# Weights of the single blocks of a mixture of experts: a second place for the first halves, and an earlier start

## The chip, the cores and the metric

One core of a Trainium2 chip runs the whole program. The metric is the time of one execution in device microseconds (us): the kernel before took 1871.33, the median of three runs (1870.01 to 1871.95). Everything is float32.

The names in the profile: PE is TensorE's matmuls and PEld its weight loads, DVE is VectorE, ACT ScalarE, POOL GpSimd, and SP SyncE, which does nothing here but issue transfers. An "SPq" line is an instruction in SP's queue. "L1367" is line 1367 of the kernel.

## The reference

There are 32 sequences of 112 tokens (3584 tokens in all) with 256 channels, and for each sequence 375 rows of context. The layer has two residual steps:

```python
x = x + tanh(g_xattn) * cross_attention(ctx, layernorm(x))   # 16 heads of 64
x = x + tanh(g_ffn) * moe(layernorm(x))

def moe(x):                                  # D = 256, F = 1024, E = 8 experts
    s = softmax(x @ gate_w)                  # (T, E)
    top2, idx = top_k(s, 2); top2 /= sum(top2)
    h = gelu(x @ w1[e] + b1[e])              # w1 (E, 256, 1024), exact gelu
    y = h @ w2[e] + b2[e]                    # w2 (E, 1024, 256)
    return sum over the two experts of top2 * y
```

The cross-attention takes its queries from the normed x, and keys and values from the normed context with the normed x behind it. Only the mixture of experts (`moe`) is touched by the change, and of it only the last part.

## The kernel before

**Order.** Nothing is scheduled by a planner around the change: each engine runs its instructions in the order in which the code writes them, and semaphores hold an instruction back until what it needs is done. A transfer is an instruction in the queue of the engine that issues it (SP, ACT or POOL), so it also stands in that engine's order; a transfer that must wait for its place in SBUF to come free holds up everything behind it in that queue.

**Stages.** The attention of the sequences comes first and takes most of the time. Each of the 3584 tokens then belongs to two experts, which makes 7168 rows; the rows are written to DRAM (`xg`) sorted by expert, padded so that the parts below line up. While the last sequences are still in attention, the kernel works out which expert each part of 256 or 128 rows belongs to (`locate_early`, `locate_late`), and the experts' rows are gone through in two kinds of units:

- 21 *pairs* (t = 0 to 20, `PAIRS = 21`): two 128-row blocks of one expert at a time, 256 rows. Both layers use a scheme with seven block products instead of eight, for which sums of the weights were written to DRAM before (`ws1`, `ws2`). One pair takes 12.94 us on PE when nothing is waited for.
- 18 *single blocks* (t = 21 to 38, `SURE = 18`) of 128 rows, called block 0 to block 17 here, in order of the experts; three more exist under a condition on a register (`tc.If(more)`).

For each unit a table in DRAM holds three numbers that are read into registers by `number(m, i, column, ...)`: the expert, the row in `xg`, and a flag that is 1 where the expert is another than that of the unit before (column 2). The flag becomes `cond` of the fetches of weights: where it is 0 the fetch is skipped, as the weights are in place.

**A single block.** `hidden(t)` (L1360 to L1376) is layer 1 in 8 features of 128, each with two matmuls (L1367) and one gelu on ACT (L1374) that adds the bias b1. `turn_rows(t + 1)` (L1158) transposes the next block's rows. `second(t - 1)` (L1382) is layer 2 of the block before: 8 matmuls of 256 columns into one bank. `combine(t - 1)` adds b2 (DVE, L1232), scales each row by its gate (DVE, L1234), and sends the rows by a scatter-add to the output in DRAM (POOL, L1207, called "the add" below). So PE's order is: hidden layer of block t, transposes for t + 1, second layer of t - 1, and so on.

**Weights of a single block.** The two layers of an expert are 1 MB each. They come in halves of 512 KB: the first half of a layer serves its features 0 to 3, the second half 4 to 7. Each half has one place in SBUF, which is taken over from the pairs' weights:

| half | place (tile) before | read by PE at |
|---|---|---|
| layer 1, first | `s23` | L1367, features 0 to 3 of `hidden` |
| layer 1, second | `12_22` | L1367, features 4 to 7 |
| layer 2, first | `t14`, under the name `b1x` | L1382, first 4 matmuls of `second` |
| layer 2, second | `b2x` | L1382, last 4 matmuls |

The profile leaves numbers out of names: `w_s` is `s23`, `w` is `12_22`, `w_t` is `t14`, `w_b2x` is `b2x`. All four are fetched on SP's queue, in `fetch_first` (layer 1, L1119) and `fetch_second` (layer 2, L1135). Such a fetch waits until PE has done with the block before in that place, and what stands behind it on SP waits too. The biases are fetched on ACT's queue (`fetch_biases`: b1 at L1074, b2 at L1077, broadcast to all 128 partitions), into two places each by turns, and so are the rows (`fetch_rows`, L1057), three units ahead (`AHEAD = 3`). The order in `run()` before, for each block t:

```python
hidden(t)
fetch_first(t + 1); turn_rows(t + 1)
second(t - 1); combine(t - 1)
fetch_second(t)
rows_ahead(t, end)
```

So layer 1 of a block is fetched when the hidden layer of the block before has let go of the places, and layer 2 of block t when the second layer of block t - 1 has. Block 0's weights come the same way: layer 1 behind the hidden layer of pair 20 (t = 20), layer 2 behind pair 20's second layer. The loop over the pairs (L1854 to L1877) has the same form, with `hidden_pair`, `second_pair` and more kinds of planes per unit.

**Two places that were free by then.** `found["w1"]` (8 KB per partition, 1 MB) holds layer 1 of pair 0, and `w2_first` (L1138, the same size, in the attention's tile `exs[2]`) layer 2 of pair 0. Both are read for the last time while pair 0 is worked on (L1185 and L1200), and are not used after that.

Of the kernel before, what the change touches and what calls it, by code (L numbers as in the profile page):

```python
# [13 lines left out]
ET = mybir.EngineType  # L14
# [9 lines left out]
def kernel(  # L24
# [20 lines left out]
    nc = tc.nc  # L45
# [155 lines left out]
    if True:  # L201
# [861 lines left out]
        def expert_of(t):  # L1063
            m, i = unit_of(t)
            e = number(m, i, 0, E - 1, (ET.SP, ET.Activation) if t > 1 else (ET.SP,))

            new = {} if t in (0, 1, EARLY, PAIRS) else {"cond": number(m, i, 2, 1)}
            return e, new
# [31 lines left out]
        def fetch_first(t):  # L1100
# [3 lines left out]
            if t < PAIRS:  # L1104
                s1_, s4_ = (
                    (n, ws1[bass.ds(e, 1), place].rearrange("o p f -> p (o f)"))
                    for n, place in (("s1", 3), ("s4", 2))
                )
                s23 = "s23", ws1[bass.ds(e, 1), 0:2].rearrange("o s p f -> p (o s) f")
                order_ = (  # L1110
                    ("11", half_of_w1(e, 0, 0)), s23, s1_, ("12_22", rows_of_w1(e, 1)), s4_
                )
            else:
                if t == PAIRS:
                    wt["11"], wt["12"] = (wt["s23"][:, n] for n in range(2))
                    wt["21"], wt["22"] = (wt["12_22"][:, n] for n in range(2))
                order_ = ("s23", columns_of_w1(e, 0)), ("12_22", columns_of_w1(e, 1))
# [3 lines left out]
        def fetch_second(t):  # L1121
# [3 lines left out]
            if t < PAIRS:  # L1125
                planes = ws2[bass.ds(e, 1)].rearrange("o (a b) p c d -> b p (o a) (c d)", b=2)
                order_ = ("b11", half_of_w2(e, 0, 0, P)), b2x, ("t14", planes[0]), ("t32", planes[1])
            else:
                if t == PAIRS:
                    wt["b1x"] = wt["t14"].rearrange("p a f -> p (a f)").rearrange(  # L1130
                        "p (c d) -> p c d", d=D
                    )
                order_ = ("b1x", half_of_w2(e, 0, 0, D)), b2x
# [6 lines left out]
        def second_ahead():  # L1140

            e, _ = expert_of(0)
            nc.sync.dma_start(w2_first, w2[bass.ds(e, 1)].rearrange("o (c p) d -> p (o c) d", p=P))

# [216 lines left out]
        def hidden(t):  # L1361
            hid[t] = found["tiles"].tile([P, NF, P], F32, tag="h", name=f"h_{t}")
            for f in range(NF):
                ps = psum(P)
                h, c = divmod(f, NF // 2)
                for k, w in enumerate((("11", "12"), ("21", "22"))[h]):
                    nc.tensor.matmul(  # L1367
                        ps,
                        lhsT=wt[w][:, c * P : (c + 1) * P],
# [8 lines left out]
        def second(t):  # L1378
            ps = psy[t, 0] = psum(D, hold=(t, 0))
            for f in range(NF):  # L1380
# [4 lines left out]
                    rhs=wt[("b1x", "b2x")[h]][:, c, :],  # L1385
# [558 lines left out]
```

## Time and profile before

| | us |
|---|---|
| median of three runs | 1871.33 |
| the profiled execution, its own time | 1865.82 |
| its span, first to last instruction | 1864.0 |
| PE busy in the span | 1843.0 |
| DVE busy | 1377.0 |
| ACT busy | 1131.8 |
| POOL busy | 969.0 |

The mean granted clock of TensorE is 0.999 of full speed, so no time goes to a throttled clock. By the page's table of DMA queues 462.51 MB go through the queues, and the core's 16 DMA engines move a mean of 248 GB/s. Block 0's hidden layer runs at 1711 us of the span, between the two layers of pair 20; pair 20's second layer ends at 1722, and the last matmul of block 17 at 1856.

How to read the lines that follow: in a *timeline* a line gives start and length in us, then the engine, the line of the kernel, the operation, output<-inputs, and how many instructions were put together (x16); in the bracket stands how long the engine had been idle before and what ended that. In a table of *stretches* a line gives the stretch, its length, then busy time and number of instructions of PE, PEld, DVE, ACT and POOL, then the granted clock, the busy share of the DMA engines and the GB/s that they moved.

### The profile page before, as it was taken

The numbers are of one execution on the slowest core, as the hardware profiler recorded it, in microseconds if no ns is written. First come the engines' busy times: TensorE is split into PE (matmuls) and PEld (weight loads), VectorE is DVE, ScalarE is ACT, GpSimd is POOL, SyncE is SP. The second block draws the span as 40 slices with busy tenths as digits, with TensorE's granted clock in tenths as the row PEclk, the third lists the DMA queues.
The fourth block names the chain that finished last, engine by engine and source line by source line (L and its number), as shares of the span: only waits on it lengthen the run. The fifth ranks groups of instructions, "written<-read, shape, count | busy, mean of one in ns | idle before, by whom it ended". The sixth has DMA issues, their size and how long they took to land. (4 is left out here: it accounts for less than half of the span.)

```text
span 1864.0 us, 37204 instructions
## 1 busy us (share of the span) xinstructions
PE 1843.0 (99%) x12336; PEld 1410.6 (76%) x12336; DVE 1377.0 (74%) x2898; ACT 1131.8 (61%) x2718; POOL 969.0 (52%) x1361
## 2 busy tenths in 40 slices
PE   8999999999999999999999999999999999999998
PEld 4667777676677677767677767777677999999887
DVE  6888887888887878788878787888776477754111
ACT  4776666666676767676767676766656344434333
POOL 6433342525354846484556655662334688877212
PEclk9999999999999999999999999999999999999999
DMA  6577767666878888989898988897548876997872
GB/s 207 203 248 250 246 215 235 222 225 205 257 272 252 305 271 275 284 283 306 275 282 276 283 289 285 261 311 241 211 171 295 269 218 179 283 347 213 247 187 42
DMA packets 389747, 462.51 MB, mean 248 GB/s; under 512 B 142984, under 2 KB 279472, under 8 KB 373168
## 3 DMA queue, kind: packets, MB, share of 16 engines
q1 hardware_dynamic: 359568, 432.19, 70.0%
q0 software_dynamic: 11328, 15.33, 4.2%
q10 hardware_dynamic: 18656, 12.58, 2.5%
q8 instruction: 99, 1.62, 0.4%
q14 instruction: 96, 0.79, 0.1%
HBM read 316.05 MB, written 186.96 MB: 270 GB/s over the span
## 5 line engine op out<-in xcount | busy, mean ns | idle before, releaser
L592 ACT ACTIVATE ex<-bank,nmx 128x512 f32<-128x512 f32 x512 | 344.0, 698 | 86.2 <-DVE nmx L583 86.2
L606 ACT ACTIVATE ex<-ex,rc 128x512 f32<-128x512 f32 x512 | 345.1, 730 | 59.4 <-DVE rc L603 58.8
L583 DVE TENSOR_REDUCE nmx<-bank 128x1 f32<-128x487 f32 x512 | 298.3, 655 | 69.8 <-PE bank L573 69.3
L611 DVE STREAM_TRANSPOSE ex<-ex 128x1024 f32<-128x1024 f32 x256 | 314.1, 1227 | 20.3 <-ACT ex L606 20.2
L524 POOL TENSOR_TENSOR vv<-tmpv,vv 128x512 f32<-128x512 f32 x64 | 82.0, 1281 | 403.9 <-ACT vv L512 393.1
L573 PE MATMUL bank<-kT,qTs 64*128 64x487 f32 x1024 | 234.2, 583 | 0.8 <-ACT outT L652 0.3
L635 PEld LDWEIGHTS bank<-exT,vv 128*64 128x64 f32 (+1 forms) x4096 | 197.5, 136 | 29.5 <-issue 24.8
L652 ACT COPY outT<-bank 128x256 f32<-128x256 f32 (+3 forms) x160 | 40.0, 314 | 289.1 <-PE bank L635 289.1
L635 PE MATMUL bank<-exT,vv 128*64 128x112 f32 (+1 forms) x4096 | 211.3, 260 | 0.0
L471 PE MATMUL bank<-tT,wkv_s 128*128 128x487 f32 x378 | 186.5, 576 | 0.5 <-ACT ex L592 0.5
L476 PE MATMUL bank<-wkv_s,tT 128*128 128x256 f32 x768 | 186.5, 379 | 0.0
L476 PEld LDWEIGHTS bank<-wkv_s,tT 128*128 128x128 f32 x768 | 145.8, 190 | 44.0 <-issue 22.5
L1452 POOL TENSOR_TENSOR piece<-piece 128x128 f32<-128x128 f32 x256 | 117.2, 458 | 109.6 <-DMA piece<-in_L_ffn_w_dram 98.3
L573 PEld LDWEIGHTS bank<-kT,qTs 64*128 64x128 f32 x1024 | 98.4, 186 | 95.8 <-issue 70.7
L1207 POOL DMA_INDIRECT out_dram<-y,xs x60 | 93.6, 1559 | 148.7 <-DVE y L1234 64.8
L476 PEld LDWEIGHTS bank<-wkv,kvT 128*128 128x128 f32 x512 | 95.8, 190 | 56.3 <-issue 33.4
L476 PE MATMUL bank<-wkv,kvT 128*128 128x256 f32 x512 | 131.7, 380 | 0.8 <-ACT ex L592 0.6
L471 PE MATMUL bank<-kvT,wkv 128*128 128x487 f32 x252 | 130.1, 598 | 0.0
L521 DVE TENSOR_TENSOR vv<-bank,vv 128x512 f32<-128x512 f32 x192 | 123.4, 668 | 6.9 <-POOL vv L524 6.9
L521 DVE TENSOR_TENSOR kT<-bank,kT 128x487 f32<-128x487 f32 x189 | 116.8, 640 | 15.5 <-PE bank L471 15.2
L1262 ACT ACTIVATE h<-h,b 128x256 f32<-128x256 f32 x160 | 66.1, 495 | 89.5 <-DVE h L1275 89.5
L410 PEld LDWEIGHTS bank<-kvT,wq_sb 128*128 128x128 f32 x512 | 96.8, 190 | 28.1 <-issue 17.0
(299 smaller groups left out, 3654.9 us busy)
## 6 DMA issues: line engine op xcount, KB each, us to landing
turned<-ex SPq DMA_DIRECT2D x128, 1024.0 KB
exT<-turned SPq DMA_DIRECT2D x128, 1024.0 KB
w_t<-ws SPq DMA_DIRECT2D x40, 512.0 KB
w<-in_L_ffn_w_dram SPq DMA_DIRECT2D x38, 512.0 KB
w_b2x<-in_L_ffn_w_dram SPq DMA_DIRECT2D x38, 512.0 KB
ws<-piece SPq DMA_DIRECT2D x64, 256.0 KB
turned_in<-inputs SPq DMA_DIRECT2D x28, 512.0 KB
kvT<-turned_in SPq DMA_DIRECT2D x224, 64.0 KB
```

Source lines behind the costliest of these rows:

```text
L410: nc.tensor.matmul(ps, lhsT=wq_sb[:, k, i * P : (i + 1) * P], rhs=kvT[g][:, k, :, :S], start=(k == 0), stop=(k == KD - 1),)
L471: nc.tensor.matmul(ps, lhsT=w[:, 0, i * P : (i + 1) * P], rhs=x[:, :NK], start=True, stop=True)
L476: nc.tensor.matmul(ps[:, c, :], lhsT=x[:, (2 * h + c) * P : (2 * h + c + 1) * P], rhs=w[:, 1, i * P : (i + 2) * P], start=True, stop=True,)
L521: nc.vector.tensor_tensor(v[o], ps, v[r], ALU.add)
L573: nc.tensor.matmul(ps[:, :NK], lhsT=qT[b // 2, i][r, b % 2].rearrange("p a i -> p (a i)"), rhs=kT[b, i][r, :], start=True, stop=True,)
L583: nc.vector.tensor_reduce(nmx[b, i][:, j : j + 1], pss[b, i][j][:, :NK], AX.X, ALU.max, negate=True)
L592: nc.scalar.activation(exs[n % EXB][:, :, p, :, j, :], ps[j].rearrange("p (c r k) -> p k c r", c=NCK, r=QW), AF.Exp, bias=nmx[b, i][:, j : ...
L606: nc.scalar.mul(t, t, rc[:, j : j + 1])
L611: nc.vector.transpose(t, t)
L635: nc.tensor.matmul(ps[y * DH : (y + 1) * DH, r, x * S : (x + 1) * S].rearrange("p (a i) -> p a i", a=QB), lhsT=vv[j // 2, c // 2][:m, c % ...
L1207: add = nc.gpsimd.indirect_dma_start(out=outf, out_offset=bass.IndirectOffsetOnAxis(ap=xs[t][:, b, D + 1 : D + 2].bitcast(I32), axis=0), i ...
L1452: nc.gpsimd.tensor_tensor(o, l, r, op) for o, l, r, op in ops
```

## The change

Single blocks no longer use `fetch_first` and `fetch_second`; these keep the pairs alone. In their place:

- `single(t)` reads the registers of block t and says where its weights lie. First halves of both layers have two places by turns: those of even blocks lie in `room[:, 0]` (in `found["w1"]`) and in the first half of `w2_first`, those of odd blocks in `s23` and `b1x` as before. Second halves keep one place each (`12_22`, `b2x`), but for block 0, whose second halves lie in the other halves of `room` and `w2_first`.
- `fetch_single(t, layer, h)` sends one half. A second half is skipped where the block's expert is that of the block before, as now; a first half, whose place last held the block before that, is skipped only where both flags, of block t and of block t - 1, are 0. Blocks 0 and 1 are always fetched.
- In the pair loop block 0's four halves go out at t = 18 (`PAIRS - 3`), behind the layer-2 planes of pair 18; block 1's layer-1 halves go out at t = 20, where block 0's layer 1 went out before.
- In `run()`, behind `hidden(t)`: the second half of layer 1 of block t + 1, then the first half of layer 1 of block t + 2. Behind `combine(t - 1)`: the second half of layer 2 of block t, then the first half of layer 2 of block t + 1. b1 of block t + 1 goes out where it did, b2 of block t + 1 where b2 of block t did, so one block earlier.

Matmuls, gelus, the work on DVE and the adds stay as they are. The instructions of the single blocks in SP's queue grow by the eight further fetches that the looser condition lets through and by the arithmetic that joins the two flags.

```diff
@@ -1064,7 +1064,7 @@
             m, i = unit_of(t)
             e = number(m, i, 0, E - 1, (ET.SP, ET.Activation) if t > 1 else (ET.SP,))
 
-            new = {} if t in (0, 1, EARLY, PAIRS) else {"cond": number(m, i, 2, 1)}
+            new = {} if t in (0, 1, EARLY) else {"cond": number(m, i, 2, 1)}
             return e, new
 
         def fetch_biases(t, e, pool, n, layers=(0, 1)):
@@ fetch_first @@
...
-            else:
-                if t == PAIRS:
-                    wt["11"], wt["12"] = (wt["s23"][:, n] for n in range(2))
-                    wt["21"], wt["22"] = (wt["12_22"][:, n] for n in range(2))
-                order_ = ("s23", columns_of_w1(e, 0)), ("12_22", columns_of_w1(e, 1))
...
@@ fetch_second @@
...
-            else:
-                if t == PAIRS:
...
-                order_ = ("b1x", half_of_w2(e, 0, 0, D)), b2x
...
@@ -1141,6 +1128,30 @@
 
             e, _ = expert_of(0)
             nc.sync.dma_start(w2_first, w2[bass.ds(e, 1)].rearrange("o (c p) d -> p (o c) d", p=P))
+
+        def single(t, cond=True):
+
+            i = t - PAIRS
+            e = number("c", i, 0, E - 1, (ET.SP, ET.Activation))
+            one = two = {}
+            if cond and i > 1:
+                one = number("c", i, 2, 1)
+                one, two = {"cond": one}, {"cond": one | number("c", i - 1, 2, 1)}
+            H = NF // 2
+            room = found["w1"].rearrange("p k (h f) -> p h k f", h=2)
+            b1x = wt["t14"].rearrange("p a f -> p (a f)").rearrange("p (c d) -> p c d", d=D)
+            wt["w1", t] = [(room[:, 0], wt["s23"])[i % 2], wt["12_22"] if i else room[:, 1]]
+            wt["w2", t] = [(w2_first[:, :H], b1x)[i % 2], wt["b2x"] if i else w2_first[:, H:]]
+            found["one", t] = e, two, one
+
+        def fetch_single(t, layer, h):
+            e, *new = found["one", t]
+            dst = wt[("w1", "w2")[layer], t][h]
+            src = columns_of_w1(e, h) if layer == 0 else half_of_w2(e, h, 0, D)
+            nc.sync.dma_start(dst, src, **new[h])
+
+        def biases_of_single(t, layer):
+            fetch_biases(t, found["one", t][0], found["weights"], 2, (layer,))
 
         def weights_ahead():
 
@@ -1363,10 +1374,10 @@
             for f in range(NF):
                 ps = psum(P)
                 h, c = divmod(f, NF // 2)
-                for k, w in enumerate((("11", "12"), ("21", "22"))[h]):
+                for k in range(KD):
                     nc.tensor.matmul(
                         ps,
-                        lhsT=wt[w][:, c * P : (c + 1) * P],
+                        lhsT=wt["w1", t][h][:, k, c * P : (c + 1) * P],
                         rhs=xsT[t][:, k, 0, :],
                         start=(k == 0),
                         stop=(k == KD - 1),
@@ -1382,7 +1393,7 @@
                 nc.tensor.matmul(
                     ps,
                     lhsT=hid[t][:, f, :],
-                    rhs=wt[("b1x", "b2x")[h]][:, c, :],
+                    rhs=wt["w2", t][h][:, c, :],
                     start=(f == 0),
                     stop=(f == NF - 1),
                 )
@@ -1854,9 +1865,15 @@
         for t in range(1, PAIRS):
             if t > 1:
                 hidden_pair(t)
-                fetch_first(t + 1)
                 if t + 1 < PAIRS:
-                    found["next", t + 2] = expert_of(t + 2)
+                    fetch_first(t + 1)
+                    if t + 2 < PAIRS:
+                        found["next", t + 2] = expert_of(t + 2)
+                else:
+                    biases_of_single(PAIRS, 0)
+                    single(PAIRS + 1)
+                    fetch_single(PAIRS + 1, 0, 0)
+                    fetch_single(PAIRS + 1, 0, 1)
                 turn_rows(t + 1, nc.scalar.copy)
                 if t + 1 < PAIRS:
                     rows_sums(t + 1)
@@ -1871,6 +1888,11 @@
             if t + AHEAD == EARLY:
                 do(outgoing)
                 del outgoing[:]
+            if t == PAIRS - 3:
+                single(PAIRS)
+                for layer in range(2):
+                    for h in range(2):
+                        fetch_single(PAIRS, layer, h)
             rows_ahead(t)
             for _ in range(2 if t == 2 or t + AHEAD > EARLY - 3 else int(t > 1)):
                 do(outgoing[:1])
@@ -1881,17 +1903,28 @@
             for t in range(begin, end):
                 hidden(t)
                 if t + 1 < end:
-                    fetch_first(t + 1)
+                    if t > PAIRS:
+                        fetch_single(t + 1, 0, 1)
+                    biases_of_single(t + 1, 0)
+                if t + 2 < end:
+                    single(t + 2)
+                    fetch_single(t + 2, 0, 0)
+                if t + 1 < end:
                     turn_rows(t + 1)
-                    if t + 2 < end:
-                        found["next", t + 2] = expert_of(t + 2)
                 if t == PAIRS:
                     second_pair(t - 1)
                     out_pair(t - 1)
+                    biases_of_single(t, 1)
                 else:
                     second(t - 1)
                     combine(t - 1)
-                fetch_second(t)
+                if t > PAIRS + 1:
+                    fetch_single(t, 1, 1)
+                if t + 1 < end:
+                    fetch_single(t + 1, 1, 0)
+                    biases_of_single(t + 1, 1)
+                if t == PAIRS:
+                    fetch_single(t + 1, 1, 1)
                 rows_ahead(t, end)
             second(end - 1)
             combine(end - 1)
@@ -1902,8 +1935,11 @@
         with tc.If(more):
             for t in range(PAIRS + SURE, PAIRS + NS):
                 fetch_rows(t)
-                fetch_first(t)
-                fetch_second(t)
+                single(t, False)
+                for layer in range(2):
+                    biases_of_single(t, layer)
+                    for h in range(2):
+                        fetch_single(t, layer, h)
                 turn_rows(t)
                 hidden(t)
                 second(t)
```

More of the change, by code (lines that the diff above doesn't have):

```diff
@@ L1103, in fetch_first @@
             fetch_biases(t, e, found["weights"], 2, (0,))
[L1104 to L1112, printed above, removed]
-            else:
-                if t == PAIRS:
-                    wt["11"], wt["12"] = (wt["s23"][:, n] for n in range(2))
-                    wt["21"], wt["22"] = (wt["12_22"][:, n] for n in range(2))
-                order_ = ("s23", columns_of_w1(e, 0)), ("12_22", columns_of_w1(e, 1))
+            s1_, s4_ = (
+                (n, ws1[bass.ds(e, 1), place].rearrange("o p f -> p (o f)"))
+                for n, place in (("s1", 3), ("s4", 2))
+            )
+            s23 = "s23", ws1[bass.ds(e, 1), 0:2].rearrange("o s p f -> p (o s) f")
+            order_ = (
+                ("11", half_of_w1(e, 0, 0)), s23, s1_, ("12_22", rows_of_w1(e, 1)), s4_
+            )
             for n, src in order_:
@@ L1124, in fetch_second @@
             b2x = "b2x", half_of_w2(e, 1, 0, D)
-            if t < PAIRS:
-                planes = ws2[bass.ds(e, 1)].rearrange("o (a b) p c d -> b p (o a) (c d)", b=2)
-                order_ = ("b11", half_of_w2(e, 0, 0, P)), b2x, ("t14", planes[0]), ("t32", planes[1])
-            else:
-                if t == PAIRS:
-                    wt["b1x"] = wt["t14"].rearrange("p a f -> p (a f)").rearrange(
-                        "p (c d) -> p c d", d=D
-                    )
-                order_ = ("b1x", half_of_w2(e, 0, 0, D)), b2x
+            planes = ws2[bass.ds(e, 1)].rearrange("o (a b) p c d -> b p (o a) (c d)", b=2)
+            order_ = ("b11", half_of_w2(e, 0, 0, P)), b2x, ("t14", planes[0]), ("t32", planes[1])
             for n, src in order_:
```

## The prediction

> **What bounds the kernel now.** I read the page's busy table first, then the stretches with their DMA share, then PE's timeline over the single blocks, then SP's, ACT's and POOL's timelines beside it. "Block n" is single block n (0 to 17), "pair n" a pair of blocks; 19 and 20 are the last pairs.
>
> The busy table: PE works in all but 21 us, and a gain can come from there alone.
> ```profile
> PE 1843.0 (99%) x12336; PEld 1410.6 (76%) x12336; DVE 1377.0 (74%) x2898; ACT 1131.8 (61%) x2718; POOL 969.0 (52%) x1361
> ```
> The stretches (length, busy time of PE, PEld, DVE, ACT, POOL, then clock, DMA share, GB/s): late pairs, the blocks up to 11, the blocks that fetch no weights, two dense pitches, pairs 18 and 19. The late pairs run the DMA engines full (1.03) and PE loses nothing; in the single blocks they are at 0.79 and PE loses 5 us.
> ```profile
> 1644.00:1696.00 52.00, 52.00 (x468) 52.00 (x468) 28.16 (x60) 22.53 (x56) 40.19 (x41) 1.00 1.03 328
> ...
> 1726.00:1816.00 90.00, 84.58 (x566) 77.42 (x565) 13.65 (x34) 30.90 (x89) 18.90 (x13) 1.00 0.79 217
> ...
> 1816.60:1845.60 29.00, 29.00 (x202) 27.34 (x201) 4.81 (x12) 11.77 (x32) 6.18 (x4) 1.00 0.29 51
> ...
> 1757.59:1766.29 8.70, 7.41 (x53) 6.79 (x51) 1.63 (x4) 3.30 (x9) 2.77 (x2) 1.00 0.96 275
> 1766.29:1773.61 7.32, 7.32 (x51) 6.91 (x52) 0.78 (x2) 2.59 (x8) 1.43 (x1) 1.00 1.06 347
> ...
> 1686.00:1701.00 15.00, 15.00 (x137) 15.00 (x136) 8.96 (x22) 5.91 (x14) 9.98 (x10) 1.00 0.70 197
> ```
> PE's timeline: where it waits, it is at the first matmul of a half of weights (in the bracket: idle time and what ended it; the 1785.90 wait names DVE, but that matmul needs nothing of that instruction, and the DMA landed then). The last two lines give the pitch of a block that waits for nothing: 7.24.
> ```profile
> 1732.14 2.02 PE L1367 MATMUL bank<-xsT,w 128*128 128x128 f32 x16 [0.73 <-DMA w<-in_L_ffn_w_dram]
> ...
> 1742.42 1.97 PE L1382 MATMUL bank<-w_t,h 128*128 128x256 f32 x8 [0.79 <-DMA w_t<-in_L_ffn_w_dram]
> ...
> 1753.73 2.02 PE L1367 MATMUL bank<-xsT,w_s 128*128 128x128 f32 x16 [0.27 <-DMA w_s<-in_L_ffn_w_dram]
> ...
> 1766.29 1.97 PE L1382 MATMUL bank<-w_t,h 128*128 128x256 f32 x8 [1.29 <-DMA w_t<-in_L_ffn_w_dram]
> ...
> 1785.90 2.02 PE L1367 MATMUL bank<-xsT,w_s 128*128 128x128 f32 x16 [1.00 <-DVE y L1234]
> ...
> 1801.79 2.02 PE L1367 MATMUL bank<-xsT,w_s 128*128 128x128 f32 x16 [1.16 <-DMA w_s<-in_L_ffn_w_dram]
> ...
> 1820.40 1.89 PE L1382 MATMUL bank<-w_t,h 128*128 128x256 f32 x8
> ...
> 1827.64 1.89 PE L1382 MATMUL bank<-w_t,h 128*128 128x256 f32 x8
> ```
> SP's timeline: 0.37 or 0.38 is a fetch that is issued, 0.07 or 0.08 one that is skipped since the expert is the block's before. So blocks 2, 3, 5, 6, 7, 9 and 11 have a new expert, the others from 1 on not. The second line is skipped at the moment its place is free; PE uses that place at 1823.86, 5.27 later: that is the time a fetch has.
> ```profile
> 1795.20 0.37 SPq L1119 DMA_DIRECT2D w_s<-in_L_ffn_w_dram  x1
> ...
> 1818.59 0.08 SPq L1119 DMA_DIRECT2D w_s<-in_L_ffn_w_dram  x1
> ```
> POOL's: the scatter-adds of the results. Each starts 0.74 after the one before has landed, 6.69 apart here ((1772.18 - 1732.04)/6), close to the pitch.
> ```profile
> 1732.04 1.55 POOL L1207 DMA_INDIRECT out_dram<-y,xs  x1 [5.67 <-DMA b<-in_L_ffn_b_dram]
> ...
> 1737.42 1.54 POOL L1207 DMA_INDIRECT out_dram<-y,xs  x1 [3.83 <-issue]
> ...
> 1772.18 1.54 POOL L1207 DMA_INDIRECT out_dram<-y,xs  x1 [6.02 <-DMA w_s<-in_L_ffn_w_dram]
> ```
>
> **What can be won.** From block 0's second layer (1726.01) to block 12's (1820.40) are 94.39 us, 12 pitches of 7.24 are 86.88: 7.51 lost. By pitch: first halves 0.96 (block 2), 0.51 and 1.46 (block 5), 1.24 (block 9), 1.40 and 0.19 (block 11), together 5.76; second halves 0.97 (block 2) and 0.43 (block 6); 0.35 in small change. Each counts a slow first matmul after the gap. Nothing else in the diff touches a wait of PE, so 7.5 us (0.4%) is the ceiling.
>
> **Part 1, two places for first halves.** SP issues them behind the second half of the block before, some 2 us after that block's hidden layer, 3.7 us of hidden and second layer short of a full pitch more than now: about 9 us ahead of use against 5.27. No first half in the trace took over 6.8 from issue to use, so the 5.76 go. But two places mean that a first half is skipped only where both of the last two experts are its own: blocks 4, 8, 10 and 12 now fetch first halves in both layers, 8 fetches of 512 KB more. In the ten pitches of blocks 1 to 10 SP issues 33 fetches instead of 26.
>
> What that asks of the DMA engines: a block without weights keeps them busy 0.29 x 7.24 = 2.1 us. The stretch 1726 to 1816 has 0.79 x 90 = 71.1, less 12.43 blocks x 2.1 = 26.1, leaves 45.0 for 28 fetches: 1.61 each. The late pairs give a lower price: 53.6 us, less 4 pairs x 4.2, over 24.5 fetches' worth of bytes: 1.50. Ten pitches then need 33 x 1.50 + 21 = 70.5 to 33 x 1.61 + 21 = 74.1 us, and at 7.24 they last 72.4: 97 to 102%, where it was 80%. The wait of the second halves is what is late next. They still have one place each, are issued when it is free, and have 5.26 (1820.38 to 1825.64). The layer-1 ones of blocks 5, 7, 9 and 11 come third behind both layer-2 fetches of the block before, all within 3.6 us. Now, the third of such a train (first halves of 9 and 11) and the one of block 5 in the dense pitch took 6.43, 6.59 and 6.78 from issue to use: mean 6.60, 1.34 too late. Four times: **5.4**. Bounds: 1.8 in all, if they land like today's second halves of these blocks (5.31, 5.55, 5.92, 6.03 by the landing records, 0.05 to 0.8 late); 11.8, if one more fetch (1.61) stands before each. I take the middle row because the count in a train stays three. The ten other second halves keep what two of them lose now: **1.4** (0 to 3).
>
> [...]
>
> **Part 2, b2 a block earlier.** ACT's fetch of b2 now goes to the slot that the combine of the block before last reads. ACT waits for DVE's L1232 (0.25 after the second layer's end, 0.42 long); behind it stand the issue of b2 and of the rows (0.35 each, with their register loads 1.3) and the eight gelus. They start about 2.1 after the hidden layer does, against 0.65 (1746.70, hidden layer at 1746.05). PE asks for the first gelu at 3.57, when the transpose takes its bank: hidden, with 1.1 left. That cover goes if the combine is late, and it waits for the add of two blocks before to have landed (its y slot; 1736.67 by the landing records against 1737.93, 1.26 to spare). Cost **0.7**, between 0 and some 12 (second rival).
>
> **Part 3, block 0's weights.** Four fetches (6.0 to 6.4 us) go out behind pair 18's, at about 1688. SP pays 4 x 0.7 and three register loads of 0.3; behind them stand the rows of block 0 (due at 1704.87, landed 1693.8 now), pair 20's first layer (skipped) and pair 19's. Between 1686 and 1701 the engines are idle 0.30 x 15 = 4.5 us; so 1.5 to 1.9 us spill over onto pair 19's last planes, which landed at 1706.78 and are due at 1708.66, 1.88 to spare: **0.3** (0 to 1.5). Block 1's weights take over the places and the time of block 0's, and have 10 us more: nothing, covered by pair 20. SP's added register arithmetic (some 0.4 per first half) lies in front of fetches with 9 us of time: nothing.
>
> **Sum.** -7.51 + 5.4 + 1.4 + 0.7 + 0.3 = +0.3 us. The profiled execution took 1865.82 (span 1864.0), 5.5 below the median of the three runs, 1871.33; the difference is put on the median: 1871.6. A measurement can tell 0.2%, 3.7 us, from no change.
>
> **Rivals.**
> Faster: the second halves land as today's (1.8, 0.5 for the others, nothing else): -5.2, 1866.1. For it: only two of today's 14 make PE wait, and the trains that delay them lose a member. Against: the engines go from 80% to full. Chance 0.25.
>
> Slower, by the adds: they are bound by their own landing. At share 1.03 one took 7.45 (started at 1701.21), a loop of 8.2. Beyond 7.24 the excess comes back each block, through y, DVE and ACT's new wait, to PE: at a loop of 8.6, 10 x 1.36 - 1.3 = 12.3 stand in place of the weights' waits: +5.1, 1876.4. It decides from about 8.4; below, slower pitches give the weights the time that they lack. For it: 6.69 leaves 8%. Against: 1688.28 landed after 6.13 in the full late pairs. Chance 0.20.
>
> Slower, by the queue: one more fetch ahead of each train: 11.8 + 1.4 + 1.0 - 7.5 = +6.7, 1878.0. For it: 102%. Against: PE's waits drain the queue. Chance 0.13.
>
> The change not doing what it says: a first half could still wait for PE. The order of SP's instructions shows them without a wait on PE past the second half ahead of them, so I leave it at nothing.
>
> **How the numbers follow.** My case, within 0.2% of before: 0.42, 1871.6, by itself 1868 to 1875. Faster 0.25, slower 0.33. Range 1865.8 to 1877.5: it holds my case, the faster rival and the first slower one, and cuts the second's outer half.
>
> **What would show it.** Right: no PE wait on the two alternating places; waits at second halves of layer 1 in blocks 5, 7, 9, 11; DMA share near 0.9 from 1726 on; 0.37 issues for first halves of blocks 4, 8, 10 and 12. Wrong: block pitches of 7.24 throughout (then the engines had room), or gelus that PE waits for (then the adds bind).

## The result, and the profile after

The changed kernel is slower: 1880.91 us median against 1871.26, ratio 1.0061 with a 95% interval of 1.0050 to 1.0072 (the two medians alone are 9.65 us, 0.52%, apart). That is above the range that was given (1865.8 to 1877.5), and on the other side of the likeliest case.

The profiled execution took 1883.44 us, its span 1881.7. Against the span before (1864.0) it is split at three places that every profile of these kernels shows: the start of pair 19's group of 24 matmuls in layer 1, the start of block 0's hidden layer, and the starts of the second layers of blocks 0 and 12.

| stretch | before | after | difference |
|---|---|---|---|
| start of the span to pair 19's x24 group | 1686.57 | 1690.36 | +3.79 |
| from there to block 0's hidden layer ("pair stretch") | 24.78 | 30.12 | +5.34 |
| block 0's hidden layer to its second layer | 14.66 | 14.67 | +0.01 |
| block 0's second layer to block 12's ("block stretch") | 94.39 | 103.27 | +8.88 |
| from there to the last group of matmuls | 33.94 | 33.94 | 0.00 |

The first row lies in the attention and the earlier pairs, which the change does not touch; other profiles (below) have anything from 1687.79 to 1694.73 there, a second one of the kernel before 1690.46. So in this profile the change costs 5.3 us at the pairs' end and 8.9 in the blocks; the forecast had 0.3 and 0. Together that is more than the times show: 9.65 us by the medians, 11.4 by the ratio, 9.2 by the ratio of e11 below. The pair stretch comes again almost to the tenth (30.04 in a second profile), so by the times the blocks' part is some 4 to 6 us. The runs e1 and e4 below leave the blocks as the change has them, and lost 3.75 and 4.69 there.

The busy table after, and the stretches that were read before (the columns are the same):

```profile
PE 1850.6 (98%) x12336; PEld 1414.8 (75%) x12336; DVE 1377.4 (73%) x2898; ACT 1123.0 (60%) x2718; POOL 969.5 (52%) x1361
```
```profile
1644.00:1696.00 52.00, 52.00 (x467) 51.94 (x466) 29.81 (x64) 21.68 (x53) 39.96 (x41) 1.00 1.05 339
1686.00:1701.00 15.00, 15.00 (x137) 15.00 (x136) 7.33 (x16) 6.71 (x17) 11.80 (x15) 1.00 0.99 303
1700.00:1726.00 26.00, 23.05 (x188) 22.46 (x187) 10.13 (x24) 9.25 (x25) 13.62 (x12) 0.93 0.72 212
1726.00:1816.00 90.00, 79.44 (x534) 72.66 (x533) 14.19 (x36) 22.96 (x82) 19.63 (x13) 0.98 0.85 233
```

PE has as many matmuls as before and is busy 7.6 us longer: some of them are slower, and the granted clock is 0.93 and 0.98 in two stretches that had 1.00. The idle share of the DMA engines between 1686 and 1701 is used up (0.99, it was 0.70), as forecast. In the blocks the share is 0.85, where the forecast had "near 0.9", and yet PE loses 10.6 us of 90.

PE's timeline after, the waits at the pairs' end and in the blocks:

```profile
1710.16 1.13 PE L1328 MATMUL bank<-w_b,h 128*128 128x128 f32 x8 [1.12 <-DMA w_b<-in_L_ffn_w_dram]
1712.53 1.16 PE L1328 MATMUL bank<-w_b2x,h 128*128 128x128 f32 x8 [1.23 <-DMA w_b2x<-in_L_ffn_w_dram]
1714.29 1.97 PE L1328 MATMUL bank<-w_t,h 128*128 128x128 f32 x8 [0.60 <-DMA w_t<-ws]
1716.05 1.91 PE L1328 MATMUL bank<-w_t,hs 128*128 128x128 f32 x8
...
1749.33 2.02 PE L1378 MATMUL bank<-xsT,w 128*128 128x128 f32 x16 [1.53 <-DMA w<-in_L_ffn_w_dram]
...
1762.74 1.99 PE L1393 MATMUL bank<-w_b2x,h 128*128 128x256 f32 x8 [2.20 <-DMA w_b2x<-in_L_ffn_w_dram]
...
1780.27 1.99 PE L1393 MATMUL bank<-w_b2x,h 128*128 128x256 f32 x8 [2.46 <-DMA w_b2x<-in_L_ffn_w_dram]
...
1794.00 0.71 PE L1378 MATMUL bank<-xsT,w 128*128 128x128 f32 x4 [0.96 <-DVE y L1243]
1795.78 0.44 PE L1169 MATMUL bank<-ident,xs 128*128 128x128 f32 x2 [1.06 <-ACT h L1385]
1796.05 3.48 PE L1393 MATMUL bank<-w_t,h 128*128 128x256 f32 x8
...
1816.62 3.61 PE L1393 MATMUL bank<-w_b2x,h 128*128 128x256 f32 x8 [2.42 <-DMA w_b2x<-in_L_ffn_w_dram]
```

What the reader is to see: no wait stands at a first half of the blocks any more (`w_s`, and `w_t` and `ex` of L1393), which was what the change could win. The waits stand at pair 19's layer-2 planes, at the second halves of *layer 2* of blocks 3, 5 and 9 (L1393, `w_b2x`), once at a second half of layer 1 (block 3, 1749.33), and at block 8 for a bank that DVE reads late and then for the gelus (1794.00 and 1795.78). The forecast named the layer-1 second halves of blocks 5, 7, 9 and 11: of these block 7 alone waits, 0.17. And in three places matmuls run at about half speed right after a wait: 3.48 and 3.61 us where 1.89 is usual, 1.91 to 1.97 where 1.06 is.

### The profile page after: what moved, and what is told of

Same layout as the page of the kernel before. It is cut to its first block, busy times and chain, and to the rows that moved or that the text cites. A ratio compares the mean times of both kernels' runs of the same rounds, so it can differ in the third digit from the quotient of the medians.

```text
span 1881.7 us, 37371 instructions
## 1 busy us (share of the span) xinstructions
PE 1850.6 (98%) x12336; PEld 1414.8 (75%) x12336; DVE 1377.4 (73%) x2898; ACT 1123.0 (60%) x2718; POOL 969.5 (52%) x1361
```

## The experiments

Times are compared with the kernel before on the same chip. Two columns give the pair stretch and the block stretch of the profiled execution.

| run | ratio to before (95%) | pair stretch | block stretch |
|---|---|---|---|
| before | 1 | 24.78 | 94.39 |
| before, second profile (e12) | 1.0003 (0.9992 to 1.0014) | 24.77 | 96.47 |
| changed | 1.0061 (1.0050 to 1.0072) | 30.12 | 103.27 |
| changed, second profile (e11) | 1.0049 (1.0037 to 1.0061) | 30.04 | 105.42 |
| e1: block 0 one pair later | 1.0028 (1.0018 to 1.0037) | 24.78 | 98.14 |
| e4: pair 20's skipped fetches left out | 1.0032 (1.0020 to 1.0045) | 25.00 | 99.08 |
| e2: b2 back in its place | 1.0013 (1.0005 to 1.0022) | 29.65 | 91.46 |
| e3: b2 from 128 rows | 1.0010 (1.0001 to 1.0019) | 29.88 | 90.79 |
| e5: e1 and e2 | 0.9989 (0.9980 to 0.9998) | 24.78 | 92.19 |
| e6: e5, b2 in DRAM for all partitions | 0.9984 (0.9975 to 0.9993) | 24.77 | 90.49 |
| e7: before, b2 from 128 rows | 0.9992 (0.9983 to 1.0001) | 24.78 | 93.18 |
| e8: e5 without the further fetches | 0.9978 (0.9968 to 0.9988) | 24.77 | 90.58 |
| e9: e6, b1 earlier | 0.9962 (0.9949 to 0.9975) | 24.78 | 90.84 |
| e10: e5, second halves in two places too | 0.9987 (0.9977 to 0.9997) | 24.78 | 92.53 |

The block stretch of one and the same kernel differs by some 2 us between its two profiles (before, and changed), so a difference of that size between single profiles says little by itself.

### Where the pair stretch went: e1 and e4

The first edit sends block 0's four halves behind pair 19's planes, not pair 18's:

```diff
-            if t == PAIRS - 3:
+            if t == PAIRS - 2:
                 single(PAIRS)
```

> The changed kernel with one edit: block 0's four halves go out one pair later, behind pair 19's layer-2 planes instead of pair 18's. In the changed kernel's profile the stretch from pair 19's x24 group of layer 1 to block 0's hidden layer is 30.12 us, before it is 24.78; from block 0's second layer to block 12's it is 103.27, before 94.39. Theory (the four transfers stand in front of pair 19's planes and hold SP, whose next fetches reuse the semaphores of transfers still under way): the first stretch falls to 24.8 to 25.5, the second stays at 102 to 104, the median at 1875 to 1876. Rival (the DMA engines are too full wherever the 2 MB go): the first stretch stays above 27, with the wait at block 0's hidden layer or at pair 20's second layer instead, and the median within 2 us of the changed kernel's 1880.9.

The pair stretch is 24.78, as before, and nothing takes its place: from block 0's hidden layer to its second layer it is 14.66. So the loss comes from the place of the four transfers in SP's order, not from the 2 MB as such. The time went to 1.0028, some 5.2 us above before; 3.75 of them stand in the block stretch (98.14). That stretch was expected at 102 to 104, since nothing in the blocks was edited: the 103.27 of the changed kernel's profile is not what every execution has.

The second edit leaves the place as it is, and every byte as well; it takes away five instructions that move nothing, the fetches of pair 20's layer 1, which are skipped when the kernel runs:

```diff
-            for n, src in order_:
+            for n, src in order_ if t != PAIRS - 1 else ():
                 nc.sync.dma_start(wt[n], src, **new)
```

> The changed kernel with one edit: the five layer-1 fetches of pair 20, which are skipped when the kernel runs since its expert is pair 19's, are left out of SP's queue; the bytes that move are the same. Theory A (SP is held: the skipped fetches wait one after another for semaphores of block 0's transfers, and pair 19's planes are issued some 8.9 us late): pair 19's planes are issued 3 to 6 us earlier, the stretch from pair 19's x24 group to block 0's hidden layer falls from 30.12 to 25 to 27 us, median 1876 to 1878. Theory B (the 2 MB in front of the planes on the DMA engines are the cause): the stretch stays at 29 to 31, median within 2 us of 1880.9.

25.00, so the bytes in front of pair 19's planes are not the cause. Two views show what is: SP's timeline of the changed kernel, with the four halves (`w` and `ex` of L1151), block 0's rows (L1057), pair 20's skipped fetches (0.07 or 0.08 each, L1113) and pair 19's planes (L1122),

```profile
1692.55 0.94 SPq L1151 DMA_DIRECT2D w<-in_L_ffn_w_dram  x2
1693.69 1.97 SPq L1151 DMA_DIRECT2D ex<-in_L_ffn_w_dram  x2
1696.41 1.94 SPq L1057 DMA_DIRECT2D xs<-xg  x1
1700.22 0.08 SPq L1113 DMA_DIRECT2D w<-in_L_ffn_w_dram  x1
1702.00 1.82 SPq L1113 DMA_DIRECT2D w_s<-ws  x2
1704.17 0.07 SPq L1113 DMA_DIRECT2D w<-in_L_ffn_w_dram  x1
1705.63 0.07 SPq L1113 DMA_DIRECT2D w_s<-ws  x1
1706.30 0.36 SPq L1122 DMA_DIRECT2D w_b<-in_L_ffn_w_dram  x1
```

and SP's waits from 1694 to 1709 (what it waited for: us in all, times, longest):

```profile
SPq L1113 <- DMA w<-in_L_ffn_w_dram: 3.0, 2, 1.6
SPq L1113 <- DMA ex<-in_L_ffn_w_dram: 1.4, 1, 1.4
```

Before, the same stretch of SP (1688 to 1702) waits mostly for PE, the five skipped fetches pass within 3.1 us, and the first plane of pair 19 follows 1.5 later:

```profile
1689.07 0.08 SPq L1119 DMA_DIRECT2D w<-in_L_ffn_w_dram  x1
...
1692.12 0.07 SPq L1119 DMA_DIRECT2D w_s<-ws  x1
1693.61 0.38 SPq L1135 DMA_DIRECT2D w_b<-in_L_ffn_w_dram  x1
```

A skipped fetch of *pair 20* waits for *block 0's* transfers, though they share no data. The semaphores in the changed kernel's trace say why: all transfer instructions of SP and ACT (1175 and 121) take eight semaphores (S100, S102 and S104 to S109) by turns, and from 1690 to 1711 us each of the 22 that take one has a wait for it ahead of it, the skipped ones too. Three of these go on 0.02 us after the transfer that had the semaphore before has landed:

```
SP goes on at   semaphore   the transfer that had it before, landed at
1700.12         S104        first half of block 0's layer 1, 1700.10
1701.90         S105        second half of block 0's layer 1, 1701.88
1703.65         S106        first half of block 0's layer 2, 1703.63
```

These three waits hold SP for 4.4 us in all.

Pair 19's first plane goes out at 1706.30, 8.9 us later than before if the 3.79 of the first row are taken off (1693.61 + 3.79 = 1697.40); PE asks for it at 1708.88. In e4 its four planes go out between 1698.83 and 1703.00, the first three still at the moment when their semaphore comes free (1698.72, 1700.69, 1702.26). Against the start of pair 19's x24 group (1688.36 there) that is 3.7 to 5.5 us earlier than in the changed kernel, and it is enough.

### Where the block stretch went: e2 and e3

The first edit fetches b2 where it was fetched before, behind the second layer of the block before, so it goes out ahead of `w_b2x`, and ACT no longer waits for DVE there:

```diff
                     second(t - 1)
                     combine(t - 1)
+                    biases_of_single(t, 1)
...
                     fetch_single(t + 1, 1, 0)
-                    biases_of_single(t + 1, 1)
```

> The changed kernel with one edit: b2 of a block is fetched where it was before, behind the second layer of the block before it, so ACT no longer waits for DVE at that fetch and the 128 KB no longer go out a block early. Theory A (the early b2 costs: it holds the gelus of block 7, and it goes out in the same instant as the second half of layer 2): of the 8.9 us that blocks 0 to 12 lost against before, at least 5 come back: 95 to 98.5 us instead of 103.27, median near 1875. Theory B (the eight further fetches fill the DMA engines, b2 is beside the point): 101 to 104, median 1879 to 1882. The wait at pair 19 stays (30 us) by both.

The second leaves b2 where the change put it, ACT's wait included, and reads 128 rows in place of one row 128 times:

```diff
-                eng.dma_start(bias[t][1], b2[bass.ds(e, 1), :].to_broadcast([P, D]))
+                one_row = b2[bass.ds(e, 1), :].to_broadcast([P, D])
+                rows_128 = w2[bass.ds(e, 1), 0:P, :].rearrange("o p d -> p (o d)")
+                eng.dma_start(bias[t][1], one_row if t < PAIRS else rows_128)
```

> The changed kernel with one edit: the blocks' b2 fetch reads 128 different rows of 1 KB (the first 128 rows of the expert's layer-2 weights) instead of one row of 1 KB 128 times; same size, same descriptors, same place in the order. The bias added to the blocks' results is therefore another one. In the changed kernel's packets, the weights crawl at 50 to 150 GB/s for some 2.5 us each time the 128 reads of one row pass. Theory A (that one row is the bottleneck): from block 0's second layer to block 12's 95 to 98.5 us instead of 103.27, no wait at a second half of layer 2 over 1 us; median near 1875. Theory B (bytes and order alone): 102 to 104, median 1879 to 1882.

91.46 and 90.79: either edit alone takes 12 to 15 us off the block stretch of the changed kernel's two profiles, 7 to 8 off that of e1 and e4, which have the early b2 as well, and both come out below before (94.39 and 96.47), more than was expected. So the change does win in the blocks, once b2 is out of its way. (With e3's edit the blocks add another bias than b2, so it is a probe and no version to use.)

What it is in the way of can be seen in the landing records. At blocks 3, 5 and 9 a first half goes out 1.4 to 2.4 us ahead of `w_b2x`, and b2 within 0.75 us of it; there `w_b2x` takes 7.64, 7.90 and 7.29 us to land, where PE asks for it after 5.5 (1762.74 - 2.20 - 1755.05). Blocks 6 and 7, which have the same b2 behind `w_b2x` but no first half within 4.7 us ahead, need 3.98 and 3.90. In e3 blocks 3, 5 and 9 need 4.47, 5.99 and 5.91, in e2 6.06, 5.99 and 5.56. The stretches show what the DMA engines do meanwhile. In the changed kernel block 10's b2 goes out at 1809.23 and block 9's `w_b2x` at 1809.29; two us of that (38 GB/s at a share of 0.62), and the passing of block 6's b2 beside block 5's `w_b2x` in e3:

```profile
1810.50:1812.50 2.00, 2.00 (x19) 2.00 (x18) 0.00 (x0) 1.84 (x8) 0.00 (x0) 1.00 0.62 38
```
```profile
1769.50:1771.00 1.50, 1.50 (x12) 1.42 (x11) 0.42 (x1) 1.12 (x5) 0.00 (x0) 1.00 1.11 299
```

By the packets, the first stretch holds the reads of the one row and next to nothing else: 1 to 28 of them start in each half microsecond and take 191 to 892 ns on average, while the weights wait. In e3 b2's packets take 46 to 48 ns on average, and 95 to 114 KB of weights move beside them in each half microsecond. Over the whole block stretch a 1 KB packet of ACT's queue takes 113 ns on average in the changed kernel, 78 before, 73 in e2 and 51 in e3. So the row is slow before too, but there b2 goes out ahead of layer 2's halves and not together with one whose window is short.

ACT's wait for DVE, which the prediction priced, is kept in e3 and costs no wait of PE's there. It costs one in the changed kernel's first profile, where an add had been held up: the fetch of b2 waits on DVE, DVE on the y slot, the y slot on an add that landed 9.26 us after its issue, and block 8's gelus start at 1795.35, 5.6 after its hidden layer (1789.75):

```profile
1784.08 1.54 POOL L1218 DMA_INDIRECT out_dram<-y,xs  x1 [9.41 <-DMA w<-in_L_ffn_w_dram]
1794.08 1.54 POOL L1218 DMA_INDIRECT out_dram<-y,xs  x1 [8.46 <-DVE y L1243]
```
```profile
1793.98 0.35 ACTq L1077 DMA_DIRECT2D b<-in_L_ffn_b_dram  x1
...
1795.35 0.63 ACT L1385 ACTIVATE h<-bank,b 128x128 f32<-128x128 f32 x2 [7.82 <-PE bank L1378]
```

In the second profile (e11) PE waits 1.91 us for block 5's gelus, but there b1 lands at 1772.53, just when ACT has come past the fetches of b2 and of the rows (1772.49). Two causes tie, and that wait can't be put down to the adds alone.

### Both edits, and the row by itself: e5, e6 and e7

> Both edits together: block 0's halves one pair later, and b2 fetched where it was before. Theory (two separate costs, each shown by its own run, that add up): the pair stretch 24.8 us as with the first edit alone, the blocks 91 to 92 us as with the second alone (before 94.39), so 2.5 to 3.5 us below the kernel before: ratio 0.998 to 0.999. Rival (what one edit frees the other stage takes, since block 0's 2 MB now land nearer to the blocks): the blocks above 93, ratio 0.9995 to 1.001.

The pair stretch is 24.78, the block stretch 92.19, 0.2 above what was expected, and the kernel is faster than before: 0.9989. The two costs are separate and add up. Half of what PE still waits for in the blocks is of another kind, and neither edit touches it: block 5's gelus are late, as their b1 landed 6.40 us after its issue (1754.00 to 1760.40), beside a half of the weights. In e4 it was 7.13, with a wait of 2.38.

```profile
1761.16 2.02 PE L1378 MATMUL bank<-xsT,w 128*128 128x128 f32 x16 [1.94 <-ACT h L1385]
```

e6 keeps both edits and writes b2 to DRAM once, for all 128 partitions:

```diff
+            nc.sync.dma_start(
+                b2d.rearrange("e p d -> p e d"), b2.unsqueeze(0).to_broadcast([P, E, D])
+            )
...
-                eng.dma_start(bias[t][1], b2[bass.ds(e, 1), :].to_broadcast([P, D]))
+                    b2d[bass.ds(e, 1)].rearrange("o p d -> p (o d)")
```

> Both edits, and b2 is written to DRAM once for all 128 partitions (1 MB, with the turned b1, in the attention), so that every later fetch of b2 reads 128 different rows; for pairs and blocks alike. Theory (128 reads of one row stop the weights wherever they pass): the blocks fall from 91.5 to 88.5 to 90.5 us, the pairs unchanged, ratio 0.9965 to 0.998 against the kernel before. Rival (once b2 stands ahead of the weights its row costs nothing more): blocks 91 to 92, ratio as with both edits alone, 0.998 to 0.999.

90.49, at the upper end of what the theory expects, while the ratio of 0.9984 fits the rival. That is 1.7 us below e5 and 1.0 below e2; e5 has the 1.94 for b1 in it and e6 has no wait for gelus, so what the row is still worth when b2 goes out ahead of the weights is not shown. In the kernel before the same row is worth little:

> The kernel before with one edit: the blocks' b2 fetch reads 128 different rows (of the layer-2 weights) instead of one row 128 times; the bias added to the blocks' results is another one. It says how much of the 7.51 us that the blocks lost before came from that row. Theory (the row slows every transfer that it meets, before too): 94.39 falls to 89 to 92 us, ratio 0.997 to 0.999. Rival (before, the row stood clear of the weights and the 5.27 us were too short by themselves): 93.5 to 95, ratio 0.9995 to 1.0005.

93.18 against 94.39 and 96.47, ratio 0.9992 with an interval that takes in 1: between the two expectations, and too little to be told from nothing.

### What the further fetches cost: e8 and e10

e8 skips a first half wherever the expert is that of the block before, so blocks 4, 8, 10 and 12 work with another expert's weights there; it is for the time alone:

```diff
-                one, two = {"cond": one}, {"cond": one | number("c", i - 1, 2, 1)}
+                one, two = {"cond": one}, {"cond": one}
```

> Both edits, and first halves are skipped wherever the block's expert is that of the block before, so the eight further fetches go; the blocks 4, 8, 10 and 12 then work with weights of another expert in their first halves. It says what the further traffic costs once b2 is out of the way. Theory of the prediction (the engines at 97 to 102% make second halves late): 91.5 falls to 88 to 89.5 us, ratio 0.996 to 0.998. Rival (the engines had room): 91 to 92, ratio as with both edits, 0.998 to 0.999.

90.58 against 91.46 (e2) and 92.19 (e5): by these single profiles the eight further fetches cost 0.9 to 1.6 us, by the medians of e5 and e8 on the same chip (11 runs each) 1.2. That is little beside the noise, but it is far from the 5.4 that the prediction had at the layer-1 second halves. The ratio is in the range of the prediction's theory, the block stretch between the two. The load was forecast well, though. DMA share times length over the block stretch is 0.91 x 92.19 = 83.9 in e5 and 0.79 x 90.58 = 71.6 in e8, so a fetch costs 12.3 / 8 = 1.54 us of all engines; the prediction had 1.50 to 1.61:

```profile
1731.25:1823.44 92.19, 88.34 (x603) 81.97 (x602) 14.44 (x36) 33.14 (x97) 20.43 (x14) 1.00 0.91 254
```
```profile
1730.84:1821.42 90.58, 88.09 (x603) 81.73 (x601) 14.48 (x36) 33.35 (x97) 20.45 (x14) 1.00 0.79 212
```

e10 goes the other way: second halves lie in two places too, and go out a block ahead (the second halves of even blocks in `room[:, 1]` and the other half of `w2_first`), 40 fetches in ten pitches.

> Both edits, and the second halves lie in two places by turns as well and go out a block ahead, so nothing has a short window any more, but 40 instead of 33 fetches go out in the ten pitches of blocks 1 to 10. By the prediction's price of 1.50 to 1.61 us of all engines for a fetch and 2.1 for the rest of a block these need 81 to 85 us, at 7.24 they last 72.4. Theory (that price holds, and the engines are the end of it): 95 to 100 us from block 0's second layer to block 12's. Rival (the price is too high, lateness comes from short windows alone): 87 to 90.

92.53, between the two theories and near neither. No wait at a weight is left in the blocks; PE waits for DVE instead, four times, two of them shown, at the same matmuls as at block 8 above (1794.00):

```profile
1748.59 0.71 PE L1378 MATMUL bank<-xsT,w 128*128 128x128 f32 x4 [0.98 <-DVE y L1243]
...
1795.54 0.71 PE L1378 MATMUL bank<-xsT,w 128*128 128x128 f32 x4 [1.38 <-DVE y L1243]
```
```profile
1779.12 1.54 POOL L1218 DMA_INDIRECT out_dram<-y,xs  x1 [6.76 <-DVE y L1243]
1786.72 1.54 POOL L1218 DMA_INDIRECT out_dram<-y,xs  x1 [6.05 <-DVE y L1243]
1795.61 1.54 POOL L1218 DMA_INDIRECT out_dram<-y,xs  x1 [7.34 <-DVE y L1243]
```

The adds from 1748.63 on stand 7.83 us apart ((1795.61 - 1748.63)/6): here the loop of the adds is what binds, with the engines at a share of 0.98 over the ten pitches. This is the prediction's first slower rival, at a higher load than the change makes.

### One more version, and the controls: e9, e11 and e12

e9 is e6 with b1 of the next block ahead of a block's gelus.

> The kernel with both edits and b2 in DRAM, and b1 of the next block goes out ahead of a block's gelus instead of behind them, some 3.5 us earlier on ACT. In the run with both edits PE waited 1.94 and 0.22 us for gelus whose b1 had landed 6.40 us after its issue. Theory (b1 is late there, and is not any more): blocks 88.5 to 90 us, ratio 0.996 to 0.998. Rival (in that run b1 was late by chance, with b2 in DRAM it isn't): 90 to 91, ratio 0.998 to 0.9990.

The block stretch is 90.84, that of e6 90.49: b1's place made no difference there. But e6 had no wait for gelus that an earlier b1 could take away; whether it would in e5, which has one, was not run. The ratio, 0.9962, is the best of all, but most of its distance to e6 (0.9984) is in the runs of before that it was compared with (1873.29, with e6 1870.62; the two versions themselves 1866.18 and 1867.71). By the stretches it wins 3.55 us against the first profile of before, 0.2%. That e9 beats e6 is not shown; that both beat the kernel before is.

> The changed kernel once more, as it is, for a second profile. If its first profile tells what the change does: 29.5 to 30.5 us from pair 19's x24 group to block 0's hidden layer, and 98 to 104 from block 0's second layer to block 12's (the runs that keep the early b2 showed 98.1 and 99.1), with waits at layer-2 second halves of blocks 5 and 9; ratio 1.004 to 1.007. If not, one of the two stretches is near that of before.

30.04 and 105.42: the second profile repeats both stretches, the second a little above what was expected, and again with waits at layer-2 second halves (1.79 to 2.88) and one of 1.91 for gelus.

> The kernel before once more, as it is, for a second profile of the blocks: the first gave 94.39 us from block 0's second layer to block 12's, and the versions with b2 back in its place 91.5 and 92.2. Theory (two places win some 2 to 4 us in the blocks once b2 is out of the way): 93.5 to 95.5 again, ratio 1.000. Rival (the first profile of before was a slow one and there is no gain): below 92.5.

96.47, above both expectations; there is a wait of 2.87 at block 6's second half of layer 1, with slow matmuls behind it, that the first profile has not. So the block stretch of one and the same kernel varies by about 2 us, and the gain of the repaired versions there is 2 to 6, by these two profiles.

## Why the prediction was wrong

**First halves (Part 1).** Right: PE waits at none of them in any version with two places. What the prediction gave back to the other halves was wrong in place and too large. The term "Four times: 5.4" for the layer-1 second halves of blocks 5, 7, 9 and 11 rests on the third of a train being 1.34 late. In the changed kernel these four lose 0.17 together, in e2 0.63, in e1 2.27 (2.03 of it at block 5); e8 puts the whole cost of the further traffic at 0.9 to 1.6. With b2 out of the way 4.6 (e2) to 5.3 us (e5) stand above 12 pitches of 7.24, where the sum left 5.4 + 1.4, and most of the waits in them are at second halves of layer 2 and at gelus. The load itself (97 to 102% of ten pitches at 7.24) was about right: e5 has 0.94 x 77.69 = 73.0 us of all engines in its ten pitches, within the 70.5 to 74.1 of the sum. A nearly full resource was taken for a late one. And one of the three rows that the 1.34 came from held more than bytes: in the dense pitch before block 5 (6.78) the row of b2 passes, from 1761.5 to 1763.5, with 168 GB/s at a share of 0.99. How much of the lateness it made is not shown: with 128 different rows (e7) that wait is 0.78 instead of 1.29, but block 9's is 1.65 instead of 1.00.

**b2 (Part 2).** This term failed by most: 0.7, "between 0 and some 12". By the block stretches e2 takes 12 to 14 us off the changed kernel, by the times 1.0061 - 1.0013 = 0.48%, 9.0 us; the same edit between e1 and e5 is worth 1.0028 - 0.9989 = 0.39%, 7.3 us. The step followed ACT's queue (wait, issue, gelus) and got it right: hidden as long as the adds are on time. It left out the transfer itself. The prediction said of every moved fetch of weights when it lands and what lands beside it, and of the 128 KB of b2 nothing, since they are a quarter of one fetch; they now go out within 0.75 us of the second half of layer 2, and are read from one row.

**Block 0's weights (Part 3).** 0.3, "0 to 1.5", was 5.3. The step counted issue times and bytes ("1.5 to 1.9 us spill over onto pair 19's last planes") and passed over "pair 20's first layer (skipped)" as work of 0.08 us each. e4 shows that these five instructions hold SP for transfers ahead of them that are still under way, three of block 0's four among them (4.4 us). PE's first wait is at pair 19's *first* plane, which by the bytes had time.

**Block 1's weights and SP's arithmetic at nothing.** Right: from block 0's hidden layer on to its second layer every version takes 14.66 to 14.69, and the arithmetic stands ahead of first halves, none of which PE waits for.

**The slow matmuls.** The prediction counted a slow first matmul behind each gap, but not a halved clock. Of the 16.39 us that the changed kernel's block stretch stands above 12 pitches of 7.24, PE's waits are 10.80 (1.53, 2.20, 2.46, 0.17, 0.96, 1.06 and 2.42); the other 5.6 are matmuls that ran slower after a wait. Two stretches at half the clock (last section) make 3.4 of these; 2.2 are left, about as much as before (7.51 less waits of 5.40). In the pair stretch a third one makes 1.7 of the 5.3.

**The rivals.** "Slower, by the adds" (1876.4) names a chain that occurs in the changed kernel, once in its first profile (in the second b1 was as late), and binds in e10; but with b2 from other rows (e3) PE waits nowhere for gelus for more than 0.10. "Slower, by the queue" (1878.0) had the waits mostly at the wrong halves. The time lay above both, since three costs came together that no rival had sized: the held queue, the row, and the slow matmuls.

Two places took all waits off the halves that have them; what they won net in the blocks is 94.39 - 91.46 = 2.9 us (e2; 5.0 against the second profile of before, 2.1 by the ratio of e5), not the 5.76 that those waits had been, since the halves without a second place then waited more.

## What to carry to other kernels

A fetch that is skipped is still an instruction with waits (three of pair 20's five held SP for 4.4 us): ahead of it in the queue, count the transfers in flight against the semaphores that they share (here eight), and send early work *behind* the last instructions that something urgent stands behind. When a small transfer is moved, ask not only what its issue waits for but which large transfer it goes out with; the broadcast from one row in DRAM was small in bytes (128 KB) and large in time (two us at 38 GB/s in the changed kernel). Fetching it ahead of the urgent one (e2) or from 128 different rows (e3) took the loss away; e6 does both, with 128 copies in DRAM. And when a resource is forecast to be 97 to 102% busy, this alone is no price: take load away or add to it (e8, e10) before giving it five microseconds.

## What the hardware showed that was not expected

- Eight semaphores are shared by SP's and ACT's transfers, and a skipped transfer waited for its semaphore as a real one did (1700.12, 1701.90 and 1703.65; pair stretch 30.12 with five such instructions, 25.00 without). With five transfers of 512 KB on the way, issuing took longer as well: 1.94 us for block 0's rows at 1696.41 (2.96 in e4), where 0.34 was usual before.
- 128 reads of one row of 1 KB were slow, and held up the weights beside them: 38 GB/s at a share of 0.62, against 299 at 1.11 with 128 different rows.
- After three of the waits in the changed kernel's profile TensorE's granted clock is 0.50, each time for 3.413 us by the clock's records, of which 1.7 are lost. This begins at 1714.44, 1796.36 and 1816.84, that is 81.92 and 20.48 us apart, 24 and 6 times 3.413: these halvings lie on a raster of that step, and begin 0.15, 0.58 and 0.22 us after a wait has ended. The lines are steps of this raster, of the changed kernel:

```profile
1711.02:1714.43 3.41, 1.58 (x12) 1.20 (x11) 0.00 (x0) 1.89 (x6) 1.22 (x1) 1.00 1.06 328
1758.81:1762.22 3.41, 1.73 (x8) 1.17 (x7) 0.42 (x1) 0.31 (x2) 0.00 (x0) 1.00 0.95 274
1775.88:1779.29 3.41, 1.93 (x10) 1.37 (x8) 0.42 (x1) 0.69 (x3) 0.00 (x0) 1.00 0.92 233
1792.94:1796.35 3.41, 1.39 (x8) 1.02 (x8) 0.94 (x3) 1.00 (x4) 1.54 (x1) 1.00 0.49 156
1813.42:1816.83 3.41, 0.99 (x5) 0.56 (x4) 0.00 (x0) 0.00 (x0) 0.00 (x0) 1.00 1.11 327
...
1796.36:1799.77 3.41, 3.41 (x10) 2.70 (x9) 0.31 (x1) 1.17 (x5) 0.00 (x0) 0.50 0.97 222
```

  In the steps ahead of the three halvings PE was busy for 1.58, 1.39 and 0.99 us, so idle for 1.83, 2.02 and 2.42. The waits of 2.20 and 2.46 in blocks 3 and 5 reach over the end of a step, which left PE busy for 1.73 and 1.93 in the first of the two (idle for 1.68 and 1.48), and no halving came; block 9's 2.42 lies within one step, and one came. In the kernel before no step from 60 us on is idle for more than 1.16, and the clock stays at 1.00 until PE's work is done. Single waits in other profiles have slow matmuls behind them too: 1.94 us at pair 19 in e2 (8 matmuls in 1.90 us where 1.06 is usual), 2.38 in e4 and 2.87 in e12 (16 in 3.65 and 3.58 where 2.02 is usual), 2.67 and 2.32 in e11 (8 in 2.96 and 3.68 where 1.89 is usual). So in the changed kernel a wait cost 1.7 us more where it left PE idle for 1.83 us or more of one step, and not where it left 1.68 or less. For a forecast: in the changed kernel's blocks 5.6 us came on top of 10.80 us of waits, 3.4 of them by the halved clock.
